# A mixture-of-experts stage with eight different sizes: experts ordered by their number of tokens, weights from an address read on the chip, zero rows stored at another time

## The chip, the cores and the metric

The kernel runs on one core of a Trainium2 chip. The metric is the device time of one execution in microseconds (us); of several runs the median is taken. The kernel before took 2926.47 us (median of three runs, 2922.64 to 2928.51).

## What is computed

Two layers over a graph of 1250 nodes with 1024 features each, all in 32-bit floats. Each layer has a graph part and a feed-forward part, both added to the running x:

```python
x = x + _L0_gnn_ref(_layernorm(x), L0_gnn_W, L0_gnn_a_l, L0_gnn_a_r, src, dst)      # attention over edges, 4 heads
x = x + _L0_ffn_ref(_layernorm(x)[None], L0_ffn_rail_maker, L0_ffn_rail_up_proj, L0_ffn_w_cproj)[0]
x = x + _L1_gnn_ref(_layernorm(x), edge_index, L1_gnn_W, L1_gnn_b)                  # normalised neighbour sum
x = x + _L1_ffn_ref(_layernorm(x)[None], ..., L1_ffn_W1, L1_ffn_W2, L1_ffn_W3, L1_ffn_Wg)[0]
```

The change is in the last line, a mixture of experts. Every token passes a shared gated network, and one of eight experts of the same form, the one whose logit is largest:

```python
def geglu(x, w1, w2, w3):
    return gelu(x @ w1) * (x @ w2) @ w3          # w1, w2: 1024 x 256, w3: 256 x 1024
idx = argmax(xf @ Wg, axis=-1)                   # one expert of 8 for each of 1250 tokens
for e in range(8):
    y = geglu(xf, W1[e], W2[e], W3[e])
    final = final + where((idx == e)[:, None], y, 0.0)
```

## The kernel before

**The stages.** Lines 198 to 384 count edges and project for the attention, lines 435 to 525 do the attention. Lines 539 to 835 are the large projection of the first feed-forward part: 16 blocks (`b`) of 49 small products (`m` from 0 to 48). Each product is four matmuls on TensorE (in the last block more), which the profile shows as eight records[...]; its sum (a tile of 128 x 626 values, 313 KB) is copied from PSUM by ScalarE (L604) into one of five buffers (`parts`) and stored by a DMA that adds to what lies in DRAM (`accumulate`, L608), issued by GpSimd. Lines 837 to 1023 are the second graph part and the eight logits per token. Lines 1029 to 1184 are the mixture of experts and the output.

**The mixture of experts.** There are 256 rows (`ROWS`) of places for each expert, of which the first 224 (`CAP`) are used. The order of the work:

- L1052 to L1079 find the expert of each token (`eq`, a one in the column of the expert).
- The shared network's first half, `hidden(hs, wsh[0], xT5, NCH, then=places)` (L1117), works on all 1250 tokens in six chunks of 32 matmul records each. After the first chunk it calls `places` (L1081).
- `places` ranks the tokens of each expert on TensorE (L1083 to L1087), turns ranks into places on VectorE (L1089 to L1102), writes each token's number to its place in DRAM by ten indirect DMAs on GpSimd's queue (L1104), and reads the list back (`tok`, L1110). A token whose rank is 224 or more is `late` (L1090); if any expert has more than 224 tokens, `flag` is set (L1114), and the branch at L1187 works those tokens out densely at the end.
- The loop over experts (L1124): load the three weight matrices, 1 MB each, by SyncE's queue (`weights`, L945 to L947; two sets of buffers); gather the tokens' rows in parts of 128 and 96 by indirect DMAs (L1131); turn them by TensorE transposes (L1137) and copies by VectorE and ScalarE (L1140); `hidden` (L1041, moving operand 128 x 224, per expert 64 records); the second projection in two parts (L1147, 16 records each), a copy by VectorE (`y`, L1150) and a store to `ys_d` by SyncE's queue (L1151).
- The shared network's second half (L1158), gathers of each token's row of `ys_d` (L1167), the sum and the output.

**Zero rows.** The gathers at L1167 name the whole of `ys_d` as their source. L781 fills what no expert stores, places 224 to 255 of each expert, with zeros: 32 rows of 4 KB, in one DMA per expert on GpSimd's queue. It stands at b = 0, m = 30 in the code, but depends on nothing but the tile `zero`; the scheduler that fixes each engine's order of instructions has placed all eight at the start of the kernel, behind the first loads of the attention's weights.

**What sets the order.** Each engine runs its instructions in one fixed order, made by a scheduler from the code's order and the dependencies. `tc.issue_after(x)` keeps an instruction behind `x` in that order. Queues of DMAs belong to the issuing engine: SyncE's (SP) for weights and stores, GpSimd's (POOL) for indirect and adding DMAs.

Of the kernel before, what the change touches and what calls it, by code (L numbers as in the profile page):

```python
# [8 lines left out]
F32 = mybir.dt.float32  # L9
F16 = mybir.dt.float16  # L10
BF16 = mybir.dt.bfloat16
I32 = mybir.dt.int32
I16 = mybir.dt.int16
AF = mybir.ActivationFunctionType
ALU = mybir.AluOpType
AX = mybir.AxisListType
# [3 lines left out]
P = 128  # L20
R, T = 125, 10
N = R * T
RA = 112
D = 1024
# [5 lines left out]
SLOPE = 0.2  # L30
EPS = 1e-5
NE = 8
CAP = 224
ROWS = 2 * P
NS = NE * ROWS // P
NP = N + 2
# [62 lines left out]
def gnn_ffn_kernel(ctx, tc, x, src, dst, gat_w, a_l, a_r, maker, up, cproj,  # L99
                   gcn_w, gcn_b, w1s, w2s, w3s, w1, w2, w3, wg, out):  # L100
    nc = tc.nc
# [21 lines left out]
    ys_d = dram.tile([NE * ROWS + 1, D], F32, name="ys_d")  # L123
    zero = const.tile([P, 1, 128], F32, name="zero")
# [73 lines left out]
    with tc.tile_pool(name="gw", bufs=1) as gwp, tc.tile_pool(name="gps", bufs=3, space=PSUM) as psp:  # L198
# [21 lines left out]
        with tc.tile_pool(name="cc", bufs=1) as ccp, tc.tile_pool(name="cw", bufs=2) as cwp:  # L220
# [9 lines left out]
            flag = ccp.tile([1, 1], I32, name="flag")  # L230
# [308 lines left out]
    with ExitStack() as tail:  # L539
# [220 lines left out]
        for n, (b, p, i, pairs) in enumerate(steps):  # L760
            m = n - 49 * b
            if n >= end - 70:

                xw[:] = [v for v in xw if v < 33]
            for w in (b, b + 1):
                while coming.get(w) and len(xw) > (0 if w == b else 16 if m < 12 else 8 if m < 20 else 4):
                    load_weights(w, *coming[w].pop(0))
            if b == 0:
                for v in first.get(m, ()):
                    hidden(0, *v)  # L770
            while j < len(sums) and sums[j][0] <= n:
                add_up(*sums[j][1:])
                j += 1
            if b == 0 and m in late:
                late_tile(late[m])
                if late[m] == T - 1:
                    xw += range(33, 41)
            if b == 0 and m == 30:

                for e in range(NE):  # L780
                    nc.gpsimd.dma_start(  # L781
                        ys_d[:NE * ROWS, :].rearrange("(p s) (a b) -> p s a b", s=NS, b=128)[CAP - P:, 2 * e + 1],
                        zero[CAP - P:].to_broadcast([ROWS - CAP, D // 128, 128]))
            if 2 <= b < 2 + HT:
                if m == 24:
                    load_pair(b - 2)
                if m == 31:
                    sum_pair(b - 2)
            if 2 + HT <= b < 6 + HT:
                if m == 24:  # L790
                    load_quarters(b - 2 - HT)
                if m == 31:
                    sum_quarters(b - 2 - HT)
            if b + 1 < NB:
                if m == 20:
                    for k in range(2):
                        load_rails(b + 1, k)
                if m in (28, 30):
                    rails(m // 2 - 14, zps.tile([P, 4, 512], F32, name="pz2")[:, 0, :P])
                if m in later:  # L800
                    hidden(b + 1, *later[m])
            assert n != end - 13 or all(v < 33 for k, v in buf.items() if k[1] == "X")
            if n in loads_at:
                load_sums(loads_at[n])
            if n == end:
                blocks.close()
                tl = rest.enter_context(tc.tile_pool(name="tl", bufs=2))
                psp = rest.enter_context(tc.tile_pool(name="tps3", bufs=2, space=PSUM))
                yh += parts
            if b == NB - 1:  # L810
                while m >= 14 and [v for v in xw if not 8 <= v < 16] and len(W3) < len(quarters):
                    load_quarter()
                if m == 23:
                    nc.gpsimd.dma_start(bias, gcn_b.partition_broadcast(R))
                while m >= 16 and len(fetched) < 4 and fetch(len(fetched)):
                    pass
                if m == 22:
                    add_out(0)
                    level(0)
                if m == 24:  # L820
                    turn_tile(0)
                if m == 27:
                    add_out(1)
                    level(1)
                    tt(bias[:, 512:], bias[:, 512:], bias[:, :512], op=ALU.subtract)
            po = product(pairs)
            if last:
                (combine if last[0] == NB - 1 else accumulate)(*last[last[0] == NB - 1:])
            for n0, k, sums_of in bring:
                if n0 <= n:  # L830
                    with tc.issue_after(added[-1]) if n > end else nullcontext():
                        for _ in range(k):
                            next(sums_of, None)
            last = b, p, i, po
# [191 lines left out]

    with back_end:
        hs = back_end.enter_context(tc.tile_pool(name="hsp", bufs=1)).tile([P, 2, N], F32, name="hs")  # L1030
        with tc.tile_pool(name="ab", bufs=2, space=PSUM) as abp, tc.tile_pool(name="tps", bufs=2, space=PSUM) as tps, \
# [49 lines left out]
            def places():  # L1081
                pr = tps.tile([R, T + 1, NE], F32, name="pt6")
                nc.tensor.matmul(pr[:, :T, :].rearrange("p a b -> p (a b)"), tri, eq.rearrange("p a b -> p (a b)"),  # L1083
                                 start=True, stop=False)
                nc.tensor.matmul(pr[:, :T, :].rearrange("p a b -> p (a b)"), one,
                                 cs[:, :T, :].rearrange("p a b -> p (a b)"), start=False, stop=True)
                nc.tensor.matmul(pr[:, T, :], one, cs[:, T, :], start=True, stop=True)  # L1087
                rank = lnp.tile([R, T + 1, NE], F32, name="rank", bufs=1)
                nc.vector.tensor_copy(rank, pr)  # L1089
                nc.vector.scalar_tensor_tensor(late, rank[:, :T, :], float(CAP), eq, op0=ALU.is_ge, op1=ALU.mult)  # L1090
                has = lnp.tile([R, T, NE], F32, name="has", bufs=1)
                nc.vector.tensor_tensor(has, eq, late, op=ALU.subtract)

                at = lnp.tile([R, T, NE], F32, name="at", bufs=1)
                nc.vector.tensor_scalar(at, rank[:, :T, :], float(P), float(1 - P * NS), op0=ALU.is_ge, op1=ALU.mult)
                nc.vector.scalar_tensor_tensor(at, rank[:, :T, :], float(NS), at, op0=ALU.mult, op1=ALU.add)
                nc.vector.scalar_tensor_tensor(at, io, float(ROWS // P), at, op0=ALU.mult, op1=ALU.add)
                nc.vector.tensor_tensor(at, at, behind.to_broadcast([R, T, NE]), op=ALU.subtract)
                nc.vector.tensor_tensor(at, at, has, op=ALU.mult)
                pf = lnp.tile([R, T], F32, name="pf", bufs=1)  # L1100
                nc.vector.tensor_reduce(pf, at, AX.X, ALU.add)
                nc.vector.tensor_tensor(place, pf, behind.rearrange("p t a -> p (t a)"), op=ALU.add)  # L1102
                for t in range(T):
                    put = nc.gpsimd.indirect_dma_start(  # L1104
                        out=tok_d, out_offset=bass.IndirectOffsetOnAxis(ap=place[:, t:t + 1], axis=0),
                        in_=own[:, t:t + 1], in_offset=None)

                    tc.declare_no_dep(put.ins, group="put", reason="rows of their own")
                    tc.add_to_no_dep_group("put", put.ins)
                nc.gpsimd.dma_start(tok, tok_d[:NE * ROWS, :].rearrange("(p s) a -> p (s a)", s=NS))  # L1110
                nc.vector.tensor_scalar(back, place, float(NE * ROWS), None, op0=ALU.min)
                most = lnp.tile([1, 1], F32, name="most", bufs=1)
                nc.vector.tensor_reduce(most, rank[0:1, T, :], AX.X, ALU.max)
                nc.vector.tensor_scalar(flag, most, float(CAP), None, op0=ALU.is_gt)  # L1114

            tok = keep.tile([P, NS], I32, name="tok")
            hidden(hs, wsh[0], xT5, NCH, then=places)  # L1117
            parts = [(s, min(P, CAP - s * P)) for s in range(-(-CAP // P))]
            w12sp.close()

            with tc.tile_pool(name="w12", bufs=2) as w12p, tc.tile_pool(name="w3p", bufs=2) as w3p, \
                    tc.tile_pool(name="xg", bufs=3) as xgp, tc.tile_pool(name="xgT", bufs=2) as xgTp, \
                    tc.tile_pool(name="hp", bufs=2) as hp, tc.tile_pool(name="yp", bufs=3, side="right") as yp:
                for e in range(NE):  # L1124
                    w12, w3t = weights((w12p.tile([P, 2, KD, F], F32, name="w12"), w3p.tile([P, 2, D], F32, name="w3t")),
                                       w1[e], w2[e], w3[e])
                    xgT = xgTp.tile([P, KD, CAP], F32, name="xgT")
                    for s, m in parts:
                        xg = xgp.tile([P, D], F32, name="xg")
# [9 lines left out]
                            eng = nc.scalar.copy if g else nc.vector.tensor_copy  # L1139
                            eng(xgT[:, 4 * g:4 * g + 4, s * P:s * P + m], pt[:, :, :m])  # L1140
                    hid = hp.tile([P, 2, CAP], F32, name="hid")
                    hidden(hid, w12, xgT, [(0, CAP)])
                    for s, m in parts:
                        po = ops.tile([P, 2, 512], F32, name="po6")
                        for f in range(2):
# [104 lines left out]
```

## Time and profile before

| | before |
|---|---|
| median of 3 runs | 2926.47 us (2922.64 to 2928.51) |
| the profiled execution | 2923.05 us |
| its span, first to last instruction | 2921.3 us |
| TensorE busy | 2857.7 us (98%), 11389 matmul records |
| VectorE, ScalarE, GpSimd busy | 1686.0, 875.8, 765.4 us |
| projection (L595) on the chain of waits | 55% of the span |
| one projection block of 49 products | 111.4 us |
| experts' loop, first matmul of the first to last matmul of the last | 2702.2 to 2875.3 us |
| of these 173.1 us TensorE busy | 167.45 us |

A row of the profile gives line, engine, operation, output and inputs, shapes, the number of such instructions, their busy time together and the mean of one, and what the engine waited for before them. Matmul records overlap[...], so what one costs is the distance between starts, not its own duration. PEld is the loading of a matmul's stationary operand. The granted clock of TensorE is 0.996 of full in the mean.

### The profile page before, as it was taken

What the parts mean: (1) busy time and instruction counts of PE and PEld (TensorE: products, weight loads), DVE (VectorE), ACT (ScalarE), POOL (GpSimd) and SP (SyncE); (2) the same over time, 40 slices, a digit from 0 to 9 for tenths busy, and PEclk for the clock granted to TensorE, in tenths of its full rate; (3) what the DMA queues carried; (4) which work ended last, traced back from release to release, by engine and by line L of the source; (5) the groups of instructions that cost most, each with busy time, mean ns of one, the idle gap of its engine ahead of it and who ended that gap; (6) DMA issues with size and microseconds to landing.
All of it is one profiled execution on the core that took longest, in us unless ns stands there. A gap on an engine that the chain in (4) does not pass through costs nothing.

```text
span 2921.3 us, 32800 instructions
## 1 busy us (share of the span) xinstructions
PE 2857.7 (98%) x11389; PEld 1892.0 (65%) x11389; DVE 1686.0 (58%) x2796; ACT 875.8 (30%) x1415; POOL 765.4 (26%) x994
## 2 busy tenths in 40 slices
PE   8999889999999999999999999999999999999998
PEld 5574777666766666666666667667667644445774
DVE  7686987855555565565465556455457665431114
ACT  2221234443343343343343443443440010010000
POOL 2000110224334334334334334344331100002001
PEclk9999999999999999999999999999999999999999
DMA  5245632569999999999999999999996502332655
GB/s 144 66 107 142 160 75 96 193 161 190 195 187 222 199 188 221 197 190 230 183 186 224 182 190 197 174 172 182 167 249 183 158 11 70 94 114 68 218 198 167
DMA packets 288438, 478.33 MB, mean 164 GB/s; under 512 B 75807, under 2 KB 159865, under 8 KB 287639
## 3 DMA queue, kind: packets, MB, share of 16 engines
q0 software_dynamic: 116176, 273.68, 52.9%
q1 hardware_dynamic: 172088, 202.44, 23.8%
q8 instruction: 95, 1.56, 0.2%
q14 instruction: 79, 0.65, 0.1%
HBM read 193.66 MB, written 282.34 MB: 163 GB/s over the span
## 4 chain that ended last, share of the span: by engine, by line
PE 80%; DMA 3%; DVE 2%; issue 0%; ACT 0%; POOL 0%; SPq 0%; DVEq 0%; ACTq 0%
PE po L595 55%; PE pab L1041 6%; PE ph L998 5%; PE po L866 4%; PE pz L429 3%; PE po L449 3%; PE po L1147 2%; DMA X<-in_gcn_w 2%; DMA yg<-ys_d,back 1%; PE pt L156 1%; PE pg L962 1%; DMA low<-in_gcn_w 1%; DMA rowbd<-st 0%; PE px L737 0%; PE pt L1137 0%
## 5 line engine op out<-in xcount | busy, mean ns | idle before, releaser
L608 POOL DMA_DIRECT2D acc_d<-low x686 | 594.6, 867 | 923.5 <-ACT low L604 895.6
L604 ACT COPY low<-po 128x626 f32<-128x626 f32 x735 | 501.2, 682 | 996.3 <-PE po L595 826.8
L595 PE MATMUL po<-X,arena 128*128 128x313 f32 x2144 | 603.5, 428 | 0.0
L595 PEld LDWEIGHTS po<-X,arena 128*128 128x128 f32 x2144 | 401.9, 189 | 170.2 <-issue 18.8
L595 PE MATMUL po<-low,arena 128*128 128x313 f32 x1584 | 449.2, 428 | 0.2 <-DVE low L588 0.2
L595 PEld LDWEIGHTS po<-low,arena 128*128 128x128 f32 x1584 | 296.8, 189 | 124.7 <-issue 13.2
L595 PE MATMUL po<-X,first_w 128*128 128x313 f32 x824 | 235.0, 429 | 0.9 <-DVE X L588 0.9
L595 PEld LDWEIGHTS po<-X,first_w 128*128 128x128 f32 x824 | 154.1, 189 | 67.0 <-issue 8.5
L595 PE MATMUL po<-X,BZ 128*128 128x313 f32 x648 | 185.8, 430 | 0.0
L588 DVE TENSOR_TENSOR X<-X 128x626 f32<-128x626 f32 x130 | 105.8, 816 | 111.1 <-PE po L595 88.2
L595 PE MATMUL po<-low,first_w 128*128 128x313 f32 x576 | 164.2, 428 | 0.9 <-DVE low L588 0.9
L595 PE MATMUL po<-low,BZ 128*128 128x313 f32 x552 | 158.4, 429 | 0.0
L595 PEld LDWEIGHTS po<-X,BZ 128*128 128x128 f32 x648 | 122.1, 191 | 50.7 <-issue 5.5
L212 PE MATMUL pz<-W,xT 128*125 128x512 f32 x320 | 141.2, 596 | 0.1
L595 PEld LDWEIGHTS po<-low,first_w 128*128 128x128 f32 x576 | 108.1, 189 | 45.8 <-issue 3.8
L595 PEld LDWEIGHTS po<-low,BZ 128*128 128x128 f32 x552 | 103.2, 189 | 44.5 <-issue 6.0
L588 DVE TENSOR_TENSOR X<-X,low 128x626 f32<-128x626 f32 x100 | 81.3, 814 | 79.8 <-PE po L595 65.2
L280 PE MATMUL pc<-os,od 125*125 125x417 f16 (+1 forms) x588 | 110.8, 344 | 4.9 <-issue 4.7
L449 PE MATMUL po<-BZ,w 125*125 125x257 f32 x400 | 95.6, 398 | 19.9 <-DVE w L447 18.8
L998 PE MATMUL ph<-low,first_w 125*125 125x512 f32 x250 | 109.5, 593 | 0.8 <-POOL tri L1066 0.8
L588 DVE TENSOR_TENSOR X<-low,X 128x626 f32<-128x626 f32 x88 | 70.9, 810 | 63.7 <-PE po L595 61.7
L588 DVE TENSOR_TENSOR low<-X,low 128x626 f32<-128x626 f32 x88 | 72.1, 820 | 60.6 <-PE po L595 59.6
(311 smaller groups left out, 3533.0 us busy)
## 6 DMA issues: line engine op xcount, KB each, us to landing
acc_d<-low POOLq DMA_DIRECT2D x735, 313.0 KB, 6.7
arena<-in_cproj SPq DMA_DIRECT2D x148, 256.0 KB
w<-in_w SPq DMA_DIRECT2D x16, 1024.0 KB
BZ<-in_cproj SPq DMA_DIRECT2D x56, 256.0 KB
first_w<-in_cproj SPq DMA_DIRECT2D x52, 256.0 KB
nm<-nm_d SPq DMA_DIRECT2D x20, 546.9 KB
w3t<-in_w SPq DMA_DIRECT2D x8, 1024.0 KB
X<-acc_d SPq DMA_DIRECT2D x19, 313.0 KB
```

The lines of the kernel that those rows point to most:

```text
L212: nc.tensor.matmul(pz, xT[:, k, t * R:(t + 1) * R], W[g][:, k], start=(k == 0), stop=(k == KD - 1))
L280: nc.tensor.matmul(pc[:, b, :nn], od[:, d - near[c][0], :], os[:, n0:n0 + nn], start=(c == win[d][0]), stop=(c == win[d][-1]))
L429: nc.tensor.matmul(pz, [*rail_parts(k)][-1][rows, :], xT[rows, (2 * b + k) % KD, n * NQ:(n + 1) * NQ], start=True, stop=True)
L449: nc.tensor.matmul(po[i], w[:, i * R:(i + 1) * R], Z[h // 2][:, s, h % 2, :], start=(s == 0), stop=(s == T - 1))
L588: tt(view(k), *a, op=ALU.add if sign == "+" else ALU.subtract)
L595: nc.tensor.matmul(po[:, o, :NQ], view(x)[:, q, o * P:(o + 1) * P], view(y)[:, q, :], start=(i == q == 0), stop=(i + 1 == len(pairs) and q ...
L604: nc.scalar.copy(part, po[:, :, :NQ])
L608: sent[:] = [nc.gpsimd.dma_start(out=acc_d[p - 1, i - 1], in_=part, accum_op=ALU.add).ins]
L866: nc.tensor.matmul(ph, block(a, x)[:, k, :], XS[W3[y, k]].rearrange("p q o -> p (q o)"), start=(k == 0), stop=(k == 3))
L998: nc.tensor.matmul(pa, cs[:, c, :], Y[FACTORS[p][1]][:, c], start=(c == 0), stop=(c == HT - 1))
L1041: nc.tensor.matmul(pab[:, :nn], w12[:, i, k, f * P:(f + 1) * P], rhs[:, k, n0:n0 + nn], start=(k == 0), stop=(k == KD - 1))
L1147: nc.tensor.matmul(po[:m, g, :], hid[:, f, s * P:s * P + m], w3t[:, f, g * 512:(g + 1) * 512], start=(f == 0), stop=(f == 1))
```

## The change

The experts are worked off in the order of how many tokens they have, most first, and the r-th of them gets 224 - 10 r places: 224, 214, 204, 194, 184, 174, 164, 154. The r-th has the rows 256 r to 256 r + 255 of `ys_d`. `places` works out each expert's rank among the eight (`pos`, ties broken by the expert's number), each expert's number of places (`cap`) and, for each position r, the expert's number (`who`). In the loop SyncE reads `who[r]` from SBUF into a register and the three weight loads take their DRAM address from it. `late` and `flag` now compare with `cap`. The chunks of `hidden`, the second part's transposes, copies, gathers and stores shrink with the number of places (96, 86, ... 26 rows).

The zero rows of the r-th position are 32 + 10 r (32, 42, ... 102). Their DMA is issued in block b = r + 1 of the projection, behind the latest adding store.

```diff
-CAP = 224
+CAP, LESS = 224, 10
+CAPS = [CAP - LESS * r for r in range(NE)]
...
-            if b == 0 and m == 30:
-                for e in range(NE):
-                    nc.gpsimd.dma_start(
-                        ys_d[:NE * ROWS, :].rearrange("(p s) (a b) -> p s a b", s=NS, b=128)[CAP - P:, 2 * e + 1],
-                        zero[CAP - P:].to_broadcast([ROWS - CAP, D // 128, 128]))
+            if 1 <= b <= NE and m == 30:
+                cap = CAPS[b - 1]
+                with tc.issue_after(sent[0]):
+                    nc.gpsimd.dma_start(
+                        ys_d[:NE * ROWS, :].rearrange("(p s) (a b) -> p s a b", s=NS, b=128)[cap - P:, 2 * b - 1],
+                        zero[cap - P:].to_broadcast([ROWS - cap, D // 128, 128]))
...
-                nc.vector.scalar_tensor_tensor(late, rank[:, :T, :], float(CAP), eq, op0=ALU.is_ge, op1=ALU.mult)
+                nc.vector.scalar_tensor_tensor(order, rank[:, T:, :], float(NE), io[:, :1, :], op0=ALU.mult, op1=ALU.subtract)
+                nc.vector.tensor_tensor(more, order.to_broadcast([R, NE, NE]),
+                                        order.rearrange("p a e -> p e a").to_broadcast([R, NE, NE]), op=ALU.is_gt)
+                nc.vector.tensor_reduce(pos.rearrange("p a e -> p (a e)"), more, AX.X, ALU.add)
+                nc.vector.tensor_scalar(cap, pos, float(-LESS), float(CAP), op0=ALU.mult, op1=ALU.add)
+                nc.vector.tensor_tensor(late, rank[:, :T, :], cap.to_broadcast([R, T, NE]), op=ALU.is_ge)
+                nc.vector.tensor_tensor(late, late, eq, op=ALU.mult)
...
-                nc.vector.scalar_tensor_tensor(at, io, float(ROWS // P), at, op0=ALU.mult, op1=ALU.add)
+                nc.vector.scalar_tensor_tensor(at, pos.to_broadcast([R, T, NE]), float(ROWS // P), at, op0=ALU.mult, op1=ALU.add)
...
+                nc.vector.tensor_tensor(seat, pos[0:1].to_broadcast([1, NE, NE]),
+                                        io[0:1, :1, :].rearrange("p a e -> p e a").to_broadcast([1, NE, NE]), op=ALU.is_equal)
+                nc.vector.tensor_tensor(seat, seat, io[0:1, :1, :].to_broadcast([1, NE, NE]), op=ALU.mult)
+                nc.vector.tensor_reduce(whof, seat, AX.X, ALU.add)
+                nc.vector.tensor_copy(who, whof)
+                nc.vector.tensor_tensor(over, rank[0:1, T, :], cap[0:1, 0, :], op=ALU.is_gt)
-                nc.vector.tensor_reduce(most, rank[0:1, T, :], AX.X, ALU.max)
-                nc.vector.tensor_scalar(flag, most, float(CAP), None, op0=ALU.is_gt)
+                nc.vector.tensor_reduce(most, over, AX.X, ALU.max)
+                nc.vector.tensor_copy(flag, most)
...
-                for e in range(NE):
+                for e, cap in enumerate(CAPS):
+                    parts = [(s, min(P, cap - s * P)) for s in range(-(-cap // P))]
+                    at = nc.values_load(who[0:1, e:e + 1], engines=(mybir.EngineType.SP,), min_val=0, max_val=NE - 1,
+                                        skip_runtime_bounds_check_because="a sum of one of 0 to 7 and zeros")
                     w12, w3t = weights((w12p.tile([P, 2, KD, F], F32, name="w12"), w3p.tile([P, 2, D], F32, name="w3t")),
-                                       w1[e], w2[e], w3[e])
+                                       *(w[bass.ds(at, 1)].rearrange("e k f -> (e k) f") for w in (w1, w2, w3)))
...
-                    hidden(hid, w12, xgT, [(0, CAP)])
+                    hidden(hid, w12, xgT, [(0, cap)])
```

More of the change, by code (lines that the diff above doesn't have):

```diff
@@ L1089, in places @@
                 nc.vector.tensor_copy(rank, pr)
-                nc.vector.scalar_tensor_tensor(late, rank[:, :T, :], float(CAP), eq, op0=ALU.is_ge, op1=ALU.mult)
+                order = lnp.tile([R, 1, NE], F32, name="order", bufs=1)
+                nc.vector.scalar_tensor_tensor(order, rank[:, T:, :], float(NE), io[:, :1, :], op0=ALU.mult, op1=ALU.subtract)
+                more = lnp.tile([R, NE, NE], F32, name="more", bufs=1)
+                nc.vector.tensor_tensor(more, order.to_broadcast([R, NE, NE]),
+                                        order.rearrange("p a e -> p e a").to_broadcast([R, NE, NE]), op=ALU.is_gt)
+                pos = lnp.tile([R, 1, NE], F32, name="pos", bufs=1)
+                nc.vector.tensor_reduce(pos.rearrange("p a e -> p (a e)"), more, AX.X, ALU.add)
+                cap = lnp.tile([R, 1, NE], F32, name="cap", bufs=1)
+                nc.vector.tensor_scalar(cap, pos, float(-LESS), float(CAP), op0=ALU.mult, op1=ALU.add)
+                nc.vector.tensor_tensor(late, rank[:, :T, :], cap.to_broadcast([R, T, NE]), op=ALU.is_ge)
+                nc.vector.tensor_tensor(late, late, eq, op=ALU.mult)
                 has = lnp.tile([R, T, NE], F32, name="has", bufs=1)
@@ L1111, in places @@
                 nc.vector.tensor_scalar(back, place, float(NE * ROWS), None, op0=ALU.min)
+                seat = lnp.tile([1, NE, NE], F32, name="seat", bufs=1)
+                nc.vector.tensor_tensor(seat, pos[0:1].to_broadcast([1, NE, NE]),
+                                        io[0:1, :1, :].rearrange("p a e -> p e a").to_broadcast([1, NE, NE]), op=ALU.is_equal)
+                nc.vector.tensor_tensor(seat, seat, io[0:1, :1, :].to_broadcast([1, NE, NE]), op=ALU.mult)
+                whof = lnp.tile([1, NE], F32, name="whof", bufs=1)
+                nc.vector.tensor_reduce(whof, seat, AX.X, ALU.add)
+                nc.vector.tensor_copy(who, whof)
+                over = lnp.tile([1, NE], F32, name="over", bufs=1)
+                nc.vector.tensor_tensor(over, rank[0:1, T, :], cap[0:1, 0, :], op=ALU.is_gt)
                 most = lnp.tile([1, 1], F32, name="most", bufs=1)
-                nc.vector.tensor_reduce(most, rank[0:1, T, :], AX.X, ALU.max)
-                nc.vector.tensor_scalar(flag, most, float(CAP), None, op0=ALU.is_gt)
+                nc.vector.tensor_reduce(most, over, AX.X, ALU.max)
+                nc.vector.tensor_copy(flag, most)
             tok = keep.tile([P, NS], I32, name="tok")
+            who = keep.tile([1, NE], I32, name="who")
             hidden(hs, wsh[0], xT5, NCH, then=places)
-            parts = [(s, min(P, CAP - s * P)) for s in range(-(-CAP // P))]
             w12sp.close()
```

## The prediction, made before the changed kernel ran

> **What bounds the kernel now.** I read the chain of waits first, then the stretch of the experts in the table by stage, the groups by shape there, and last the order of time around the rows that the change touches. The chain is TensorE nearly throughout, in the experts' loop too:
>
> ```profile
> PE 80%; DMA 3%; DVE 2%; issue 0%; ACT 0%; POOL 0%; SPq 0%; DVEq 0%; ACTq 0%
> ```
>
> The same chain in order of time, around the loop (start, duration, work, records with their loads):
>
> ```profile
> 2702.22 12.37 PE pab L1041 x64
> 2724.91 12.26 PE pab L1041 x64
> 2745.71 12.13 PE pab L1041 x64
> ...
> 2854.53 12.38 PE pab L1041 x64
> 2875.48 5.16 PE po L1158 x12
> 2885.41 5.93 DMA yg<-ys_d,back
> ```
>
> One expert is some 21.6 us (2702.2 to 2875.3 for eight), 12.3 of them its first half, and the last line says that behind the loop the gathers of `ys_d` take over. In the loop TensorE is busy 167.45 of 173.1 us, so the matmuls' own length sets it. What one matmul costs is read from the order of time:
>
> ```profile
> 2643.24 56.21 PE L1041 MATMUL pab<-xT,w12s 128*128 128x417 f32 x160
> ...
> 2745.46 12.03 PEld L1041 LDWEIGHTS pab<-xgT,w 128*128 128x128 f32 x64 [0.29 <-issue]
> 2745.54 12.30 PE L1041 MATMUL pab<-xgT,w 128*128 128x224 f32 x64
> ```
>
> 417 columns come every 56.21 / 160 = 351 ns, 224 columns every 12.03 / 64 = 188 ns: 0.84 ns a column, and nothing fixed on top.
>
> **The first halves.** The eight experts lose 0, 10, ... 70 columns, 280 together, in 64 records each: 64 x 280 x 0.84 ns = 15.05 us, all on the path. That holds only if nothing else than the columns sets the pace at 154 columns, where the sum wants 129 ns. The suspect is the loading of the stationary operand: its row is 188 ns too, with no gap between loads, as if loading were the bound already. By that row the gain would be nothing. Loads between shorter matmuls decide it:
>
> ```profile
> 2642.67 0.19 PEld L1083 LDWEIGHTS pt<-eq,tri 125*125 125x125 f32 x1 [0.16 <-issue]
> 2642.78 0.30 PEld L1085 LDWEIGHTS pt<-cs,one 125*125 125x125 f32 x2
> 2642.99 0.30 PEld L1087 LDWEIGHTS pt<-cs,one 125*125 125x125 f32 x2
> 2643.21 0.30 PEld L1041 LDWEIGHTS pab<-xT,w12s 128*128 128x128 f32 x2
> ```
>
> Five loads start in 2643.21 - 2642.67 = 0.54 us, one every 108 ns, between matmuls of 80 and 8 columns; each shows 0.19 us because records overlap. So the floor is 108 ns, under 129, and the 15.05 us stand.
>
> **Transposes and copies.** The second part's eight transposes per expert shrink from 96 to 26 columns. Here a rule speaks against a gain: the Trainium skill, page "TensorE: Matmul & The Clock Gate", section "LDWEIGHTS (loading the stationary operand)", has a load cost its columns / 1.2 in ns whatever its rows; a transposed block keeps 128 columns, 107 ns, so nothing would be saved. The trace has eight 96-row transposes in 0.83 us with the last record 0.25 long, (0.83 - 0.25) / 7 = 83 ns apart, so below the rule; by the row 8 x 280 x 0.84 = 1.9 us go at most. But little of it lies on the path: with one PSUM buffer for the second projections, the second part waits for VectorE's copy `y` of the first (1.23 us), which covers the transposes between. After the second part, every other expert waits 1.94 us (2766.10 to 2768.04) for `y` (1.22) and then VectorE's `xgT` copy, 0.54 us for 384 columns. That copy shrinks by 1.1 ns a column (0.69 us for 512): 0.04, 0.13, 0.22 and 0.31 us, 0.7 together. The other experts lose a trailing transpose, some 0.15 us each, 0.45. I take 1.15 us; ends 0 and 3.
>
> **The last store.** From the issue of the last `ys_d` store (2876.8) to the first gather (2880.9) are 4.2 us. Its 96 rows of 4 KB took 0.16 us each, six in turn on each of 16 DMA engines, 1.0 us; 26 rows are two in turn, 0.3. I take 0.5 us; ends 0 and 0.7. What follows, ten gathers and ten outputs, has the same rows and is only moved.
>
> **Places and weights.** VectorE has eight more small operations ahead of `place` (each 0.13 to 0.27 us apart), 2 us, and `who` is ready at about 2647.6 (the ranks are there at 2643.4). Behind `place` wait ten indirect stores on POOL, `tok`, and the first gathers; these were issued from 2665.5 and landed about 7 us later, and TensorE first wants them at 2699.3, when the shared first half is done. Cover over 20 us: nothing. On SP the read of `who` stands ahead of all weight loads; before, the first two experts' six loads were issued from 2617.4 to 2631.9. Now they wait for 2647.6; behind them on SP stand only the flag's read and later weights and stores. 6.3 MB at 299 GB/s (the table's stretch from 2622 to 2641, in which they landed) are 21 us, landed by 2669 where 2702 is needed: cover 33 us, nothing; uncovered it would cost those 21 us. They now run beside `tok`'s stores and gathers, which have the 20 us. Later reads stand behind a `ys_d` store with 11 us before the next weights may start (2746.9 to 2757.9). Weights are issued some 31 us before use, now some 27, and land in about 12. DMA needs some 15 us of each expert's 21.6, and of 17.9 at the shortest. I take 0; ends 0 and +3.
>
> **Zero rows.** At the start eight stores leave POOL (0.64 us each, 17.1 to 24) and the DMAs, whose share was about 1 there. TensorE's one wait in that stretch, 0.60 us at 22.9, is for ScalarE's copies: 0, ends -0.5 and 0. In the projection one store per block now stands between two adding stores on POOL. Three rows bear on it:
>
> ```profile
> L608 POOL DMA_DIRECT2D acc_d<-low x686: 856/865/1796, 635.5 to 2195.1; - x172
> DMA to landing us min/median/max: 2.6/6.7/10.7
> ```
>
> ```profile
> DMA to landing us min/median/max: 2.3/3.2/4.9
> ```
>
> ```profile
> 966.90:1078.20 111.30, 111.30 (x462) 76.50 (x461) 63.92 (x95) 43.90 (x68) 43.91 (x53) 1.00 1.09 202
> ```
>
> The first two lines are the adding stores, the next is the old zero stores, the last a whole block (length, busy times of PE, PEld, VectorE, ScalarE, POOL, clock, DMA share, GB/s). Five buffers at 2.27 us a product give 11.4 us; less ScalarE's copy, an adding store may take 10.5 us to land before ScalarE waits, and 12 before TensorE does (two PSUM tiles). It takes 7.1 in such a block, up to 10.7 where counts are loaded beside it, and TensorE is busy 111.30 of 111.30 us. A zero store of 102 rows, 0.16 to 0.25 us each over 16 engines, is 1.0 to 1.6 us. POOL is busy 44 of 111 us. Cost 0.
>
> The rule against it: page "DMA: Bandwidth & Descriptors", section "Why a DMA increments its semaphore by 16 and not by 1": the engines of a DMA are the largest number up to 16 that divides its slowest dimension, with an exception for some direct copies from GpSimd. 62 and 82 rows would go over 2 engines, 92 over 4, 102 over 6; at 0.25 us a row 7.9, 10.4, 5.8 and 4.3 us in turn. Against the 4.9 us of slack (12 - 7.1) TensorE would stop 3.0 + 5.5 + 0.9 = 9.4 us. The nearest row is GpSimd's load of 125 rows, which by the division gets 5 engines, a share of 0.31:
>
> ```profile
> 227.00:229.00 2.00, 2.00 (x6) 0.94 (x5) 0.26 (x1) 0.59 (x1) 0.00 (x0) 1.00 1.03 225
> ```
>
> That is `els` under way (issued 224.5) with a DMA share of 1.03: all engines. I take 0; ends 0 and +9.4. The rule also narrows SP's `ys_d` stores (86 rows over 2 engines, 43 x 0.16 = 6.9 us), off the path by 10 us or more; the last, 26 rows over 13, is the same two in turn.
>
> **The sum.** 15.05 + 1.15 + 0.5 = 16.7 us off a span of 2921.3: 2904.6; with the 1.75 us around it, the profiled execution goes from 2923.05 to 2906.35. The median of the runs lay 3.4 us above that execution, so 2926.5 - 16.7 = 2909.8 us. About 0.2%, 5.9 us, is what a measurement here can tell from no change.
>
> **The rivals.**
> *Loading sets the pace.* If 188 ns is the floor, only 1.65 us go: 2924.8, no change. For it: the row without gaps. Against: five loads in 0.54 us. 4%.
> *Zero stores narrow, with slack.* 16.7 - 9.4 = 7.3 us: 2919.2, just faster. For it: the divisors; against: the row of `els`. 7%.
> *Zero stores narrow, with no room to drain.* A DMA share of 1.04 to 1.09 can mean that the engines never catch up. Then delays add up from block to block: 7.9 + 10.4 + 5.8 + 4.3 and 4.8 for the even ones are 33 us, less the 4.9 once, 28 us of stop in blocks 4 to 8: 2938, slower. It decides from 22.6 us on (16.7 + 5.9). Against it: adding stores land in 10.7 us beside loaded counts and are back at 7 in the next block, so they do drain. 5%.
> *The experts don't fit.* If the r-th expert had over 224 - 10 r tokens, the branch at L1187 runs all experts densely: per expert 192 records at 351 ns and 80 at 428, some 100 us, over 800 in all. From the reference's inputs I count 204, 201, 198, 161, 143, 132, 127 and 84 tokens, all under 224, 214, ... 154. 2%.
> *Late weights.* From the register's read, each expert 1 to 2 us late: gain 2 to 8 us, about 2921. 2%.
>
> **How the numbers follow.** The forecast has 80%, by itself 2905 to 2915 (gains 13 to 20, and 1 to 2 us of runs). Faster: 80 + 5 of the slack case; same: 4 + 2 + 2; slower: 5 + 2. The range reaches to the slack case, 2904 to 2920.
>
> **What would show it.** Right: L1041's records in the eighth expert 129 to 130 ns apart; periods falling from 21.6 to about 17.5 us; projection blocks at 111.4 us with no ScalarE wait for a DMA; first transposes of the loop still at the end of the shared half. Wrong: loads 188 ns apart at 154 columns; ScalarE's copy L604 waiting for DMA in blocks 4 and 6; adding stores landing in over 12 us; TensorE waiting for `w` in the loop.

## The result, and the profile after

In 20 runs each, the changed kernel took 2930.7 us in the median (2927.88 to 2938.52) and the kernel before 2925.7 (2922.36 to 2936.05): a ratio of 1.0021, 95% interval 1.0015 to 1.0027, so 5.0 us slower. The forecast was 2909.8. The profiled execution took 2930.6 us (before 2923.05), its span 2928.9.

Numbers of lines have moved: the products are L596, ScalarE's copy L605, the adding store L609, the zero stores L783, the first halves L1044, the output's gather L1194.

The chain of waits is still TensorE, but DMAs have 4% of it where they had 3%:

```profile
PE 80%; DMA 4%; DVE 2%; issue 1%; ACT 0%; POOL 0%; POOLq 0%; DVEq 0%; ACTq 0%
```

In order of time (start, length, work) the chain shows both halves of the story. Before, no block of the projection had such a line of `acc_d`:

```profile
968.32 61.40 PE po L596 x232
1035.78 18.71 DMA acc_d<-low
1055.32 6.14 PE po L596 x16
...
1268.38 19.86 DMA acc_d<-low
1289.07 7.02 PE po L596 x16
...
1500.89 13.11 DMA acc_d<-low
1514.83 4.49 PE po L596 x16
...
2725.01 12.37 PE pab L1044 x64
2747.59 11.79 PE pab L1044 x64
2767.86 11.04 PE pab L1044 x64
...
2865.45 8.64 PE pab L1044 x64
2879.24 3.56 PE po L1174 x8
2887.90 7.63 DMA yg<-ys_d,back
```

The first halves fall from 12.4 to 8.6 us, as forecast; but the loop begins at 2725.0 instead of 2702.2, and an adding store that took 18.7 us to land, then one of 19.9, stands in the way of the products. The sum over the profiled executions: the loop starts 22.8 us later, the stretch from there to the first gather is 15.8 us shorter (178.7 to 162.9), the rest 0.6 longer, 7.6 in all. Of the 22.8, 3.6 are there when the projection's first product starts (512.1 against 508.5), which varied from 508.1 to 513.2 over all runs below but one (told there), without a pattern. Most of the rest comes from the blocks of the projection.

The table by stage, for blocks 3, 4 and 6 (length, then busy times of PE, PEld, VectorE, ScalarE, POOL, then granted clock, DMA share, GB/s):

```profile
854.80:966.10 111.30, 111.30 (x462) 76.49 (x460) 64.72 (x95) 43.84 (x68) 45.05 (x54) 1.00 1.09 205
966.10:1085.80 119.70, 113.11 (x462) 77.57 (x461) 63.03 (x93) 43.83 (x68) 46.48 (x54) 0.97 1.04 191
1197.10:1320.30 123.20, 113.89 (x461) 78.07 (x460) 66.53 (x97) 43.74 (x68) 47.64 (x54) 0.96 1.00 186
```

Taken from the starts of the products, a block that doesn't stop is 111.36 us long. Block 4, with the zero store of 62 rows, is 8.3 us longer, block 6 (82 rows) 11.9, block 8 (102 rows) 0.5, all others nothing: 20.7 us. The profiled execution before has 2.7 us of longer blocks too (7, 9 and 10, cause not looked for), so the blocks account for 18.0 of the 22.8 us. Part of the 20.7 is not waiting: PE is busy 1.8 and 2.6 us longer in blocks 4 and 6, at a mean clock of 0.97 and 0.96.

The same place in the order of time, with what each waited for in brackets, and cut into four-microsecond pieces:

```profile
1033.67 2.39 POOL L783 DMA_DIRECT2D ys_d<-zero  x1
1035.78 1.20 POOL L609 DMA_DIRECT2D acc_d<-low  x1
...
1054.59 0.68 ACT L605 COPY low<-po 128x626 f32<-128x626 f32 x1 [10.06 <-DMA acc_d<-low]
1055.32 4.03 PE L596 MATMUL po<-X,BZ 128*128 128x313 f32 x8 [6.59 <-ACT low L605]
```

```profile
1046.00:1050.00 4.00, 2.73 (x16) 1.44 (x14) 0.00 (x0) 0.00 (x0) 0.00 (x0) 1.00 1.08 208
1050.00:1054.00 4.00, 0.00 (x0) 0.00 (x0) 0.00 (x0) 0.00 (x0) 0.00 (x0) 0.73 0.60 114
1054.00:1058.00 4.00, 2.68 (x5) 1.84 (x6) 2.49 (x4) 2.24 (x4) 1.44 (x2) 0.50 0.64 103
```

The adding store behind the zero store is issued at 1035.8 and lands only near 1054.5, 2.2 us after the zero store's last packet is done (1052.3). ScalarE, whose five buffers are then all under way, waits 10.1 us for it, and TensorE 6.6 us for ScalarE. From 1050 to 1054 no engine does anything, while the DMAs are 0.60 busy. Over the projection ScalarE waits for adding stores twelve times (total, times, longest); in the profile before it never does:

```profile
ACT low L605 <- DMA acc_d<-low: 40.0, 12, 12.8
```

The zero stores themselves, and the adding stores' landing in the projection (10.7 us at the most before):

```profile
L783 POOL DMA_DIRECT2D ys_d<-zero x8: 947/1620/2591, 699.6 to 1499.3; - x8
```

```profile
DMA to landing us min/median/max: 4.5/6.9/20.6
```

In the trace's records of single DMA packets, the 62 rows were under way for 13.4 us with 1.66 packets at once in the mean, the 82 rows for 16.4 us with 1.89, which I read as two engines. Between 1042 and 1050 us, 10 to 13 packets of adding stores are under way beside the 1.8 to 1.9 of the 62 rows: the other engines go on with later stores. The stores of 32, 42, 52, 72, 92 and 102 rows took 1.9, 2.9, 2.1, 3.5, 6.3 and 7.0 us.

### The profile page after: what moved, and what is told of

Its sections match the earlier page's. It is cut to its first block, busy times and chain, and to the rows that moved or that the text cites. A ratio compares the mean times of both kernels' runs of the same rounds, so it can differ in the third digit from the quotient of the medians.

```text
span 2928.9 us, 32871 instructions
## 1 busy us (share of the span) xinstructions
PE 2852.2 (97%) x11389; PEld 1881.2 (64%) x11389; DVE 1689.3 (58%) x2806; ACT 872.8 (30%) x1415; POOL 772.0 (26%) x994
## 4 chain that ended last, share of the span: by engine, by line
PE 80%; DMA 4%; DVE 2%; issue 1%; ACT 0%; POOL 0%; POOLq 0%; DVEq 0%; ACTq 0%
PE po L596 55%; PE ph L1000 5%; PE pab L1044 5%; PE po L868 4%; PE pz L430 3%; PE po L450 3%; PE po L1174 2%; DMA acc_d<-low 2%; DMA yg<-ys_d,back 1%; PE pt L157 1%; PE pg L964 1%; DMA rowbd<-st 0%; PE pt L1164 0%; PE px L738 0%; DMA arena<-in_gcn_b 0%
## 5 line engine op out<-in xcount | busy, mean ns | idle before, releaser
L609 POOL DMA_DIRECT2D acc_d<-low x686 | 589.4, 863 | 931.1 <-ACT low L605 907.0
L605 ACT COPY low<-po 128x626 f32<-128x626 f32 x735 | 500.5, 681 | 1013.1 <-PE po L596 813.2
L596 PE MATMUL po<-X,arena 128*128 128x313 f32 x2144 | 603.5, 428 | 0.0
L596 PEld LDWEIGHTS po<-X,arena 128*128 128x128 f32 x2144 | 401.9, 189 | 170.2 <-issue 18.3
L596 PE MATMUL po<-low,arena 128*128 128x313 f32 x1584 | 449.6, 428 | 0.4 <-ACT low L605 0.4
L596 PEld LDWEIGHTS po<-low,arena 128*128 128x128 f32 x1584 | 297.3, 190 | 125.2 <-issue 12.9
L596 PE MATMUL po<-X,first_w 128*128 128x313 f32 x824 | 234.9, 429 | 0.0
L596 PE MATMUL po<-X,BZ 128*128 128x313 f32 x648 | 190.2, 438 | 15.9 <-ACT low L605 15.9
L596 PEld LDWEIGHTS po<-X,first_w 128*128 128x128 f32 x824 | 154.1, 189 | 66.0 <-issue 8.5
L596 PEld LDWEIGHTS po<-X,BZ 128*128 128x128 f32 x648 | 124.5, 195 | 68.4 <-ACT low L605 16.9
L596 PE MATMUL po<-low,first_w 128*128 128x313 f32 x576 | 164.1, 428 | 0.0
L596 PE MATMUL po<-low,BZ 128*128 128x313 f32 x552 | 158.4, 429 | 0.0
L596 PEld LDWEIGHTS po<-low,first_w 128*128 128x128 f32 x576 | 108.1, 189 | 44.8 <-issue 3.8
L596 PEld LDWEIGHTS po<-low,BZ 128*128 128x128 f32 x552 | 103.2, 189 | 44.5 <-issue 6.0
L589 DVE TENSOR_TENSOR low<-X 128x626 f32<-128x626 f32 x89 | 72.7, 820 | 60.8 <-PE po L596 48.9
```

What stands on the lines that cost most here:

```text
L589: tt(view(k), *a, op=ALU.add if sign == "+" else ALU.subtract)
L596: nc.tensor.matmul(po[:, o, :NQ], view(x)[:, q, o * P:(o + 1) * P], view(y)[:, q, :], start=(i == q == 0), stop=(i + 1 == len(pairs) and q ...
L605: nc.scalar.copy(part, po[:, :, :NQ])
L609: sent[:] = [nc.gpsimd.dma_start(out=acc_d[p - 1, i - 1], in_=part, accum_op=ALU.add).ins]
```

## The experiments

*The theory:* a zero store in this form, in which each row is eight times the same 512 bytes, goes over as many DMA engines as the largest number up to 16 that divides its rows (the rule that the prediction cites; 62 and 82: two); the adding stores behind it use those two as well and wait for them. *Rivals:* any zero bytes put at this place do it, by their amount; their place in POOL's queue does it; or the new places, the register and the order of the experts take the time.

**Rows rounded up.** The change, with 32, 48, 64, 64, 80, 96, 96, 112 rows of zeros (more bytes than the change, all multiples of 16):

```diff
-                cap = CAPS[b - 1]
+                cap = ROWS - -(-(ROWS - CAPS[b - 1]) // 16) * 16
```

> The changed kernel with each zero store rounded up to a multiple of 16 rows (32, 48, 64, 64, 80, 96, 96, 112; the rows too many are stored over later by the experts). Theory 'few engines' (a store of 62 or 82 rows runs on 2 of 16 DMA engines, 31 and 41 rows one behind the other, and the adding stores queue behind it): no ScalarE wait for an adding store, all blocks 111.4 us, 20.7 us less than the changed kernel, about 2910 us. Rival 'any store there' (GpSimd's issue of up to 2.6 us and the bytes delay the adding stores, however they are spread): more rows than before, so 2930 us or more. Rival 'beside the count stores' (the delay is the meeting with the stores of the counts' sums at m = 31): little changed, 2928 to 2932 us.

Measured: 2906.8 us against 2923.4 (0.9935, 0.9922 to 0.9949): 16.7 us faster. Its waits in the projection, and its zero stores:

```profile
ACT low L605 <- DMA acc_d<-low: 1.8, 1, 1.8
```

```profile
L783 POOL DMA_DIRECT2D ys_d<-zero x8: 965/1081/1197, 699.4 to 1480.9; - x8
```

With more bytes at the same place in the same queue the loss is gone, but for one stop of 1.9 us in block 4 of this profile. Amount and place are ruled out as its cause.

**The zero stores' part alone.** The kernel before, with the change's zero stores (first), and with its own 32 rows moved into blocks 1 to 8 (second):

```diff
-            if b == 0 and m == 30:
+            if 1 <= b <= NE and m == 30:
...
+                cap = CAP - 10 * (b - 1)     # first kernel
+                cap = CAP                    # second kernel
+                with tc.issue_after(sent[0]):
```

> The kernel before with zero stores of 32, 42, ... 102 rows in blocks 1 to 8, the experts as before. If the zero stores are the whole loss: 20.7 us more than before, 2946 us, with stops of about 8 us in block 4, 12 in block 6 and under 1 in block 8. If the loss needs the rest of the change: 2926 us.

> The kernel before with its eight zero stores of 32 rows each moved into blocks 1 to 8, and nothing else. Few engines: 32 rows go over 16 engines, no stop, 2925.7 us within 0.1%. Any store there: in proportion to rows, 256 of 536, half of 20.7 us, about 2936 us. Beside the count stores: blocks 2 to 6 stop by a few us each, 2930 to 2940 us.

Measured: 2943.1 us (1.0067, 1.0051 to 1.0083), 19.7 slower, with stops of 8.3 and 11.7 us in blocks 4 and 6; and 2921.2 us (0.9991, 0.9983 to 0.9999), no loss. The loss comes from the sizes, whatever else is changed.

**The rest alone.** The change with 224 places for every expert (`LESS = 0`): register, ranks among experts and order remain, no sizes shrink.

> The changed kernel with 224 places for every expert (the ladder's step 0), so 32 zero rows each: what is left is the experts' order, the places' ten more operations on VectorE, the register's read and the loads from its address. My prediction: all covered, time as with the moved zero stores alone, 2921 to 2926 us, experts' loop 173.1 us. Rival 'late weights': each expert 1 to 2 us later, 2930 to 2940 us.

Measured: 2923.2 us against 2923.2 (0.9996, 0.9988 to 1.0005). They cost nothing.

**62 rows, in two forms.** The kernel before with 62 rows in each of blocks 1 to 8, once as repeated zeros and once as plain rows of 1024 values from another tile:

```diff
+                cap = ROWS - 62
...
-                        zero[CAP - P:].to_broadcast([ROWS - CAP, D // 128, 128]))
+                        zero[cap - P:].to_broadcast([ROWS - cap, D // 128, 128]))              # repeated
+                        ys_d[:NE * ROWS, :].rearrange("(p s) d -> p s d", s=NS)[cap - P:, 2 * b - 1], xT[cap - P:, 0, :D])   # plain
```

> The kernel before with a zero store of 62 rows in each of blocks 1 to 8 (rows that experts use too are stored over later). Few engines: every store runs on 2 engines, 31 rows one behind the other, and stops TensorE for about 8 us, also in blocks 1, 7 and 8, where no count stores are near: 66 us more, about 2990 us. Any store there: 496 rows, fewer than the 536 of the change, so about 20 us more, 2945 us. Beside the count stores: stops in blocks 2 to 6 only, about 40 us more, 2965 us, and blocks 1, 7, 8 at 111.4 us.

> As the run before it, 62 rows in each of blocks 1 to 8, but each store is plain rows of 1024 values out of another tile (the turned activations) instead of eight repeats of 128 zeros; what lands in these rows is never read, the output is the same. If the number of engines follows from the number of rows alone: 2 engines again, about 2990 us. If it was the repeated zeros that kept the store from all engines (the load of 125 rows that I took for the nearest row has no such repeat): no stops, 2926 us. If the loss were the descriptors of the repeats: also less, under 2950 us.

Measured: 2997.5 us (1.0249, 1.0224 to 1.0275) and 2922.9 us (0.9999, 0.999 to 1.0008), against 2923.2. Their zero stores, repeated first, with ScalarE's waits (total, times, longest):

```profile
L782 POOL DMA_DIRECT2D ys_d<-zero x8: 2104/2363/2382, 696.0 to 1545.2; - x8
...
DMA to landing us min/median/max: 16.8/19.6/22.4
```

```profile
ACT low L604 <- DMA acc_d<-low: 96.0, 16, 13.4
...
PE po L595 <- ACT low L604: 59.0, 8, 10.0
```

and plain:

```profile
L782 POOL DMA_DIRECT2D ys_d<-xT x8: 865/868/876, 697.3 to 1477.6; - x8
...
DMA to landing us min/median/max: 6.9/7.7/8.0
```

```profile
ACT low L604 <- DMA acc_d<-low: 6.0, 4, 3.5
```

Same rows, bytes, place and queue: 74 us in the one form, nothing in the other. So it is the number of rows *and* the form together that make a store narrow: 1.5 to 1.8 of its packets at once in the mean, against 3.2 to 4.3 of the plain ones. The issue on POOL is longer too (2.36 us against 0.87). The eight stops of the first are 7.0 to 12.1 us, longest in blocks 2 to 5 (10.8 to 12.1); blocks 1, 7 and 8, with no counts beside them, stop too (7.0, 7.6 and 9.4), so the meeting with the counts isn't what makes a stop.

The two forms differ in more than the repetition. In the trace's records of the instructions the repeated store counts 62 rows of 8 pieces of 512 bytes, the plain one 62 pieces of 4096. The `els` load, the prediction's nearest row, counts 125 pieces of 10000 bytes, and its source is repeated too: it reads one row of 9.8 KB 125 times (`partition_broadcast` at L190), as the sizes in the list of DMAs before show:

```profile
els<-rowel POOLq DMA_DIRECT2D x2, 1220.7 KB, 10.3
...
rowel<-st POOLq DMA_DIRECT2D x2, 9.8 KB, 1.6
```

Still 15.5 to 15.9 of its packets were under way at once (227 to 231 us). So a repeated source alone doesn't make a DMA narrow; what the narrow ones have and the others don't is several pieces in a row, here repeated.

**The change with plain rows.** The change's own sizes, as plain rows (diff as above):

> The changed kernel with its own row counts (32, 42, ... 102) and places, each store as plain rows of 1024 values out of the turned activations instead of repeated zeros (the rows are never read, the output is the same). If the repeat in the pattern is what narrows the store: all engines, no stops, as with the rounded stores, 2905 to 2910 us. If 62 and 82 rows need rounding in this kernel: 2928 us or more.

Measured: 2907.3 us against 2924.1 (0.9947, 0.9934 to 0.9961), the profiled span 2904.1. The forecast's sum of spans was 2904.6. Its sizes from 42 to 102 rows, none a multiple of 16, cost nothing in this form.

**61 rows.** As the 62 repeated rows, with a prime number, which by the theory is one engine (`cap = ROWS - 61`):

> The kernel before with a zero store of 61 rows in each of blocks 1 to 8: one row fewer than in the run with 62, but a prime number, so one engine, 61 rows one behind the other. Few engines: from the depths seen (23 rows deep no stop, 31 rows 7 to 12 us, 41 rows 12 us) some 0.4 us a row, 18 to 25 us a block, 150 to 190 us in all, about 3090 us. If the count of rows matters and not the depth per engine: as with 62, about 2997 us.

Measured: 3048.9 us (1.0426, 1.0406 to 1.0445): 125 us slower where 62 rows cost 74. One row fewer and 50 us more speak for few engines and against the amount. The trace has 0.9 to 1.0 of the store's packets at once in the mean, so one engine. The size fell short of a doubling: eight stops of 13.1 to 18.2 us, mean 15.9. ScalarE's waits:

```profile
ACT low L604 <- DMA acc_d<-low: 145.1, 16, 19.0
```

**SyncE's queue.** The 62 repeated rows issued by SyncE, behind a weight load, so that no adding store stands behind them in their queue:

> 62 rows in each of blocks 1 to 8 again, but issued by SyncE, whose queue holds weight loads and no adding stores. If the adding stores are late because they stand behind the narrow store in the same queue: no or small stops, 2926 to 2940 us. If they are late because 2 engines are taken from every queue: stops as large as from GpSimd's queue, about 2990 us.

Measured: 3076.0 us (1.0515, 1.0499 to 1.0531), worse than either theory said. TensorE's waits in the projection:

```profile
PE po L596 <- DVE low L589: 58.4, 5, 15.2
PE po L596 <- ACT low L605: 37.0, 6, 7.7
PE po L596 <- DVE X L589: 16.1, 2, 12.9
```

The longest are now for VectorE's sums, and ScalarE still waits for adding stores (71.5 us, 13 times). That the queue's order alone makes the stop is thus refuted; but the run isn't clean, since here the trace shows the same rows as packets of 512 bytes and not of 4096, and a store is under way for 28 to 34 us, against 12 to 17 from POOL. How much is due to that wasn't separated.

**The old place.** The change with its own sizes, but all eight stores at b = 0, and the same with rounded sizes:

```diff
-            if 1 <= b <= NE and m == 30:
+            if b == 0 and m == 30:
...
+                for e, cap in enumerate(CAPS):
+                    cap = ROWS - -(-(ROWS - cap) // 16) * 16     # second kernel only
```

> The changed kernel with the zero stores at their old place, free for the scheduler to put at the start, in their new sizes. All three theories: the projection's stops go; the experts' loop keeps its 15.6 us. Few engines: 62 and 82 rows are narrow at the start too, but only loads that are not waited for stand behind them, so 2910 to 2913 us. If something else of the change costs (the read of the expert's number, the places), the time stays above 2915 us.

> The changed kernel with the rounded zero stores at their old place at the start. Few engines: the 14 us that the narrow stores cost there (a start of the projection at 535 instead of 519 to 522 us) go, about 2908 us. If it was the place or the bytes (2.4 MB instead of 1) that cost there: 2915 to 2925 us.

Measured: 2927.5 us against 2923.4 (1.001, 1.0 to 1.002), a miss; and 2908.8 against 2924.1 (0.9945, 0.9931 to 0.9958). In the first the projection starts at 524.7 us instead of 508.5, in the second at 509.8 (the expectation's 535 and 519 to 522 are counted from 10.5 us earlier). The first one's zero stores on POOL, VectorE's wait for the first inputs (2 times, 12.1 us the longest; 2.5 before), and the first 100 us of it (PE busy 79.74, against 89.36 before):

```profile
19.60 8.62 POOL L782 DMA_DIRECT2D ys_d<-zero  x5 [0.35 <-DMA W<-in_gat_w]
```

```profile
DVE st L142 <- DMA xt<-in_x: 14.6, 2, 12.1
```

```profile
0.00:100.00 100.00, 79.74 (x320) 49.97 (x321) 68.77 (x193) 18.79 (x40) 22.92 (x68) 0.93 0.48 122
```

I had taken the start to be free, since the old 32-row stores were free there. Narrow ones hold up the input, and the projection starts 16.2 us later. With rounded sizes old and new place differ by 0.9945 to 0.9935, less than their intervals: the move to the blocks by itself neither gains nor costs.

## Why the prediction was wrong, point by point

The eighth expert's transposes and the loads of its first half, in order of time:

```profile
2863.90 0.67 PE L1164 MATMUL pt<-ident,xg 26*128 26x26 f32 x8
2865.45 8.41 PEld L1044 LDWEIGHTS pab<-xgT,w 128*128 128x128 f32 x64 [0.98 <-DVE xgT L1167]
```

- **First halves.** Right. 64 records in the eighth expert stand (8.41 - 0.19) / 63 = 130.5 ns apart, where 129 to 130 were forecast: loading isn't the floor at 154 columns. By the starts of all their records the first halves lose 14.9 us, where 15.05 were forecast.
- **Transposes and copies.** Forecast 1.15 us. The stretch's 15.8 us less the first halves' 14.9 and the last store's 0.3 leave some 0.6. Eight transposes of 26 columns take 0.67 us, (0.67 - 0.215) / 7 = 65 ns apart against 83 for 96 columns: a smaller fall than by columns, and still below the rule's 107 (an estimate from the page that the prediction cites). The term is small. From one first half to the next the last two periods are 18.2 and 19.0 us, where the prediction had them fall to about 17.5.
- **Last store.** From its issue to the first gather 3.84 us against 4.16: 0.3 of the forecast 0.5. It varied: 3.0 in the changed kernel with plain rows.
- **Places and weights.** Right at nothing: the kernel with `LESS = 0` is within 0.1% of the one before.
- **Zero rows: the step that failed.** It read: "The nearest row is GpSimd's load of 125 rows [...] all engines. I take 0; ends 0 and +9.4." The runs put 20.7 us of stops there, outside both ends. Two things were wrong in it.
  - *The row was not near.* The load of `els` has one piece of 10000 bytes a row, the zero stores eight pieces of 512. One piece a row takes more than two engines in a store as well (62 plain rows, no stop), so it isn't the direction that tells the two apart. Nor is it repetition as such: `els` is itself a repeated source, as shown under the 62 rows, and goes over all engines. The Trainium skill, "DMA: Bandwidth & Descriptors", section "Why a DMA increments its semaphore by 16 and not by 1", allows an exception to its rule of divisors for "some direct copies" from GpSimd; here the copies with one piece a row behave like the exception, and the zero stores with eight follow the rule (62 and 82 rows: two engines; 61: one). Whether it is the second counted dimension or the repetition within the row wasn't tried.
  - *The upper end was mis-sized.* The rival "with slack" had the right mechanism but 0.25 us a row (its 7.9 and 10.4 us should by that be 7.8 and 10.3). Under load it was 13.4 / 31 = 0.43 us and 16.4 / 41 = 0.40. With the measured times and the forecast's own slack of 4.9 us, 62 rows stop 13.4 - 4.9 = 8.5 us (measured 8.3), 82 rows 16.4 - 4.9 = 11.5 (11.9), 92 rows 6.3 - 4.9 = 1.4 (0), 102 rows 7.0 - 4.9 = 2.1 (0.5): 23.5 against 20.7. With 23.5 in the sum the forecast would have been 6.8 us slower, with the measured 20.7 it is 4.0; 5.0 was measured.
- **The rival "no room to drain"** came nearer in time (2938), but not by its mechanism: delays didn't add up. Blocks 5 and 7, behind the stops, are 111.36 us long.
- **The sum.** With the narrow stores taken away, by rounding or by plain rows, the gain is 16.7 and 16.8 us, where the sum said 16.7. That it fits to a tenth is luck: the intervals of these two ratios allow 15 to 23 and 11 to 19 us.

**What stays open.** Why a stop behind 62 rows is 7 us in one block and 12 in another: in every block it is 4.0 to 5.4 us shorter than the time that the store itself was under way (11.7 to 16.6 us), which is the slack again, but why the store took longer in some blocks was not tested. Why one engine isn't twice as slow as two: the 61 rows were under way for 17.3 to 22.5 us, 0.28 to 0.37 us for each row in turn, against 0.38 to 0.54 for the 31 rows in turn of the 62; why a row took less there isn't known. Open too are which part of the zero stores' form makes them narrow, and what part of SyncE's loss is its smaller packets. Of all kernels run, the change with rounded rows or with plain rows is the fastest, 16.7 us below the kernel before, and the rounded rows at the old place (15.3 below) can't be told from them. The rounded form, which needs only the tile of zeros, is the one to use.

## What to carry to other kernels

When a change alters how many rows a DMA has, ask first over how many engines its pattern goes: a GpSimd store whose rows are several repeated pieces did well here with multiples of 16 rows (and with 42, 52 and 72), even though rounding up wrote more than was needed, and badly with 62, 82 or 61. A narrow DMA is paid for by the wide ones behind it, so price it by its time under load less the buffers' slack, and look for it where the queues are full. And a row of the trace is near only if it has the same pattern: a copy with one piece a row, repeated or not, said nothing about one with eight.

## What the hardware showed that was not expected

- Issuing a narrow store holds POOL longer: 2.4 us for 62 repeated rows and 3.8 for 61 (3.5 to 3.8), against 0.95 for 32 and 0.87 for 62 plain ones.
- After a stop of TensorE the granted clock falls: in block 4 to 0.73 in the four microseconds of the stop and 0.50 in the next four, and TensorE is busy 1.8 and 2.6 us longer in the blocks with a stop (113.11 and 113.89 us against 111.30). I read that as the price of the slower clock, on top of the wait; it wasn't tried by itself.
- The same pattern issued by SyncE went out in 512-byte packets and cost 153 us, twice what it cost from POOL.
